# Two tables of slots instead of one: five expert blocks filled from the first twelve token tiles and run in pieces inside the last tiles' stages

## The chip, the cores and the metric

The kernel runs on one NeuronCore of a Trainium2 chip. The metric is the device time of one execution in microseconds. The engines are named as in the profile: PE is TensorE (PEld its weight loads), DVE is VectorE, ACT is ScalarE, POOL is GpSimd, SP is the sync engine, which here only issues DMAs. All data are float32.

## The reference, cut to what matters

The input is x (2, 1024, 256), so 2048 tokens of width 256, and a context ctx (2, 77, 256). Four residual sublayers follow each other, each behind a layer norm (`a` to `d` are the names that the kernel gives them).

```python
x = x + cross_attention(layernorm(x), ctx, ctx, mask)      # a: 16 heads of 16
x = x + routed_attention(layernorm(x))                     # b: 4 of 16 heads of 64, chosen per batch, 1024 keys
x = x + gelu(layernorm(x) @ ctx.T) @ ctx                   # c: feed-forward on the context
x = x + moe(layernorm(x))                                  # d

def moe(x):                                # E = 8 experts, H = 256, F = 1024
    logits = x @ w_router
    probs = softmax(logits); sel = argmax(probs); wgt = probs[sel]
    for e in range(8):
        h = relu(x @ w1[e] + b1[e])
        y = h @ w2[e] + b2[e]
        out += (sel == e) * wgt * y
```

Each token goes to one expert only. How many tokens an expert has is known only when all logits are there.

## The kernel before, in words

**Tiles.** A token tile is 128 tokens; there are T = 16, handled in groups of two (c and d stages) or in 32 steps of stage b (`b_step`, one step for a pair of heads and a stretch of queries). `xs[:, t, :]` holds the residual stream of tile t in SBUF.

**Order.** On PE, DVE, ACT and POOL the instructions run in the order in which the Python code issues them (`tc.manual_schedule`). A small plan places side work inside the steps of stages a and b: `at(stage, step, pos, f, args)` registers a call, and `take` runs it at that position. Only SP, the DMA queue of weights and of the rows written to DRAM, is ordered by the tile framework's scheduler. Waits between engines are inserted by the framework from the tiles that instructions read and write.

**Stages c and d inside b.** When the queries of a group of two tiles are through stage b, its group runs c and d some steps later: `do_rows("c")` (layer norm: statistics on DVE, the power −1/2 on POOL, the rows y on POOL or DVE), `do_turn` (transposes on PE), `c_hidden`, `c_gelu`, `c_out`, then the same for d, where the rows y and xs also go to a DRAM table `ztok` of 2 × 256 numbers a token, then `d_logits` (PE) and `d_expert` (DVE: argmax as a one-hot `oh`, running counts `seen`). The last group, tiles 14 and 15, ends after the last b step.

**Table of slots.** With all 16 tiles through d, two matmuls (`rank_ps`, L1051 and L1055) give every token's rank within its expert and the counts. DVE turns them into the number of 128-token blocks of each expert, the block's expert (`eidi`), and each token's slot (L1061 to L1145). 16 one-hot matmuls (`tok_ps`, L1124; each shows as two records in the profile) invert this into lists: for each block slot its token (`tok`) and weight (`swgt`). Experts' last blocks may be partly empty; at most NB = 23 blocks arise, 20 always run, and the rest stand in an If.

**Expert blocks.** `pipeline(range(used), block_loads, block_hidden, block_out)` runs the blocks as a three-stage pipeline: in one step the weights of block n + 2 are asked for, block n + 1 does its hidden part, and block n its output part.

- `block_loads` (L1151): w1s and w2s (1 MB each) and b2s (128 KB, the bias spread over partitions) on SP, and zb, an indirect gather of 128 rows of `ztok`, on POOL. Three buffers for weights, four for zb.
- `block_hidden` (L1172): the block's bias b1s, two transposes of zb (`ybps`), a copy (`ybT`), then 8 × 2 matmuls into one PSUM tile `ph` of 128 × 1024 (f counts the 8 slices of 128 hidden units), then eight relus from `ph` into `ehT`:

```python
        for f in range(FC):
            for c in range(C):
                nc.tensor.matmul(
                    ph[:, f, :], lhsT=ws[n][0][:, c, f * P : (f + 1) * P], rhs=ybT[:, c, :],
                    start=(c == 0), stop=(c == C - 1),
                )
        for f in range(FC):
            if f < FC // 2:
                nc.scalar.activation(hT[:, f, :], ph[:, f, :], AF.Relu, bias=b1s[:, f : f + 1])
            else:
                nc.vector.tensor_scalar(hT[:, f, :], ph[:, f, :], b1s[:, f : f + 1], 0.0, ALU.add, ALU.max)
```

- `block_out` (L1202): 8 matmuls of `ehT` by w2s into `epo` (128 × 256), two DVE operations into `ob` (bias, then weight and residual), and an indirect scatter of `ob` to the output on POOL.

A matmul of the program shows as two records on PE in the profile. PSUM has three pools of two buffers: `big` (ph), `trp` (transposes), `accp` (epo and most others).

Of the kernel before, what the change touches and what calls it, by code (L numbers as in the profile page):

```python
# [39 lines left out]
def kernel(  # L40
# [55 lines left out]

    const = ctx.enter_context(tc.tile_pool(name="const", bufs=1))
# [7 lines left out]
    work = ExitStack()  # L105
    ytp = work.enter_context(tc.tile_pool(name="ytp", bufs=2))
    ynp = work.enter_context(tc.tile_pool(name="ynp", bufs=6))
    ap_ = work.enter_context(tc.tile_pool(name="ap_", bufs=2))
    wsp = work.enter_context(tc.tile_pool(name="wsp", bufs=1))
    qkp = work.enter_context(tc.tile_pool(name="qkp", bufs=2))  # L110
    stage_a = ExitStack()
    rawp = stage_a.enter_context(tc.tile_pool(name="rawp", bufs=1))
# [7 lines left out]
        nm: rawp.tile([P, C, D], F32, name=f"raw_{nm}") for nm in "qkvo"  # L120
# [11 lines left out]
    def bcast_load(name, ap, n):  # L132
        t = const.tile([P, n], F32, name=name)
        nc.sync.dma_start(t, bcast_rows(ap, n))
        return t

    def col_load(name, ap):
        t = const.tile([P, C], F32, name=name)
        with nc.allow_non_contiguous_dma(reason="bias columns"):
            nc.sync.dma_start(t, ap.rearrange("(c p) -> p c", p=P))  # L140
        return t
# [7 lines left out]
    mask_i = const.tile([P, B, KC], I32, name="mask_i")  # L149
# [6 lines left out]
    bv_b = bcast_load("bv_b", a_bv, D)  # L156
# [3 lines left out]
    bo_b = bcast_load("bo_b", a_bo, D)  # L160
# [28 lines left out]
    hmask = const.tile([P, HG], F32, name="hmask")  # L189
# [12 lines left out]
    hsel = const.tile([P, NCH, H], F32, name="hsel")  # L202
# [15 lines left out]
    hwin = const.tile([P, NCH, HW], F32, name="hwin")  # L218
# [3 lines left out]
    neg3 = const.tile([P, 1], F32, name="neg3")  # L222
# [10 lines left out]
    ones16 = const.tile([P, P], BF16, name="ones16")  # L233
# [45 lines left out]
    def ln_rows(tag, t0, bias=None, y_out=None, last=False):  # L279
# [4 lines left out]
        nc.gpsimd.tensor_tensor(rs, rs, minus_half, ALU.pow)  # L284
        ys = []
        for i in range(2):
            y = ynp.tile([P, D], F32, name=f"y_{tag}_{t0 + i}", tag="y")
            (nc.vector if last else nc.gpsimd).tensor_scalar(  # L288
                y, xs[:, t0 + i, :], mv[:, i, 0:1], rs[:, i : i + 1], ALU.subtract, ALU.mult
            )  # L290
            ys.append(y)
            if y_out is not None:
                r0 = (t0 + i) * P
                nc.sync.dma_start(y_out[r0 : r0 + P, :D], y)
                nc.sync.dma_start(y_out[r0 : r0 + P, D:], xs[:, t0 + i, :])
        if bias is not None:
            add_bias(t0, 2, bias)
# [35 lines left out]
    def turn_weight(nm):  # L333

        t = wT[nm] = const.tile([P, C, D], F32, name=f"w{nm}T")
# [9 lines left out]
    keep01 = const.tile([P, B, KC], F32, name="keep01")  # L345

    mneg = const.tile([P, B, HG, KC], BF16, name="mneg")

    kblk = const.tile([P, B, C, HG, KC], F32, name="kblk")

    def context_k(m):
# [9 lines left out]
        kT = small.tile([P, B, KC], F32, name=f"kT_{m}", tag="kT")  # L361
# [6 lines left out]
    vc = const.tile([KC, B, D], F32, name="vc")  # L368
    pick = const.tile([KC, 3, KC], F32, name="pick")
    nc.gpsimd.tensor_copy(pick, ident[:KC, :KC].unsqueeze(1).to_broadcast([KC, 3, KC]))  # L370
    vblk = const.tile([P, B, NCH, HW, HD + 1], F32, name="vblk")
# [168 lines left out]
    def route_mean(b):  # L540
        ys = small.tile([P, C], F32, name=f"yt_{b}", tag="yt")
        nc.vector.tensor_reduce(ys, sel[b], AX.X, ALU.add)
        ym = sel[b] = small.tile([P, C, P], F32, name=f"ym_{b}", tag="ym", bufs=1)
# [17 lines left out]
    def route_heads(b):  # L561
# [54 lines left out]
        hot = small.tile([P, NA, NH], F32, name=f"hot_{b}", tag="hot", bufs=1)  # L616
# [4 lines left out]
        hb = small.tile([P, 2, NA, NH], F32, name=f"hb_{b}", tag="hb", bufs=1)  # L621
# [4 lines left out]
        hs_ = small.tile([P, 2, NP, 2], F32, name=f"hs_{b}", tag="hs", bufs=1)  # L626
# [10 lines left out]
    def b_qk(b, k, m, n):  # L637

        w, bc, _ = sel[b]
        if (b, k, m) not in qks:  # L640
            qks[b, k, m] = qkp.tile([P, S], F32, name=f"{k}T_{b}_{m}", tag=f"{k}T{m}")
        ps = accp.tile([P, 512], F32, name=f"bps_{b}_{m}_{k}_{n}", tag="acc")
# [8 lines left out]
        return lambda: nc.scalar.activation(  # L651
# [4 lines left out]
    def b_v(b, t):  # L656
        w, _, bv = sel[b]
        if b not in vs:
            vs[b] = qkp.tile([P, NT, NA, FD], F32, name=f"v_{b}", tag="v")
        ps = trp.tile([P, NA, FD], F32, name=f"vbps_{b}_{t}", tag="tr")  # L660
# [151 lines left out]
    def c_gelu(t0):  # L812
# [3 lines left out]
        nc.scalar.activation(g, ps, AF.Square)  # L816
        nc.vector.scalar_tensor_tensor(g, g, 1 / GELU_C, ps, ALU.add, ALU.mult)
        nc.scalar.activation(g, g, AF.Tanh, scale=math.sqrt(2 / math.pi) * GELU_C)
        nc.vector.scalar_tensor_tensor(g, g, 1.0, ps, ALU.add, ALU.mult)
# [25 lines left out]
    emx = keep.tile([P, T], F32, name="emx")  # L845
    TE2 = [P, 2, E]
    lps = {}

    def d_logits(t0):
        yT = yTs.pop(("d", t0))  # L850
        ps = lps[t0] = accp.tile([P, 2, E], F32, name=f"elps_{t0}", tag="acc")
        for i in range(2):
            for c in range(C):
                nc.tensor.matmul(
                    ps[:, i, :], lhsT=yT[:, c, i * P : (i + 1) * P], rhs=wrt_s[:, c, :],
                    start=(c == 0), stop=(c == C - 1),
                )

    def d_expert(t0):

        ts_ = slice(t0, t0 + 2)
        nc.vector.tensor_copy(logits[:, ts_, :], lps.pop(t0))
# [25 lines left out]

    rows = {}
# [9 lines left out]
    def do_rows(tag, t0, *args):  # L899
        rows[tag, t0] = ln_rows(tag, t0, *args)  # L900

    def do_turn(tag, t0, pool=trp, ptag="tr"):

        b, n = t0 // NT, t0 % NT * P
        if tag in "ab":
            if (tag, b) not in yTs:
                yTs[tag, b] = ytp.tile([P, C, S], F32, name=f"yT_{tag}{b}", tag="yT")
# [6 lines left out]
    def do_qk(*args):  # L914
        b_qk(*args)()
# [43 lines left out]
    for s, args in (  # L959
# [3 lines left out]
        at("a", s, 3, do_qk, *args)  # L963
    at("b", 3, 3, do_qk, 0, "q", 0, 512)
    at("b", 5, 3, do_qk, 0, "q", 1, 512)
    for t in range(NT):
        at(*(("a", 18, 3), ("a", 18, 3), ("b", 0, 3), ("b", 0, 3),
             ("b", 1, 0), ("b", 1, 3), ("b", 2, 0), ("b", 2, 3))[t], b_v, 0, t)
    for s, pos, args in (
        (6, 3, ("k", 0, 0)), (7, 2, ("k", 0, 512)), (8, 2, ("q", 0, 0)), (9, 2, ("k", 1, 0)),  # L970
        (9, 3, ("k", 1, 512)), (10, 3, ("q", 1, 0)), (17, 2, ("q", 0, 512)), (21, 2, ("q", 1, 512)),
    ):
        at("b", s, pos, do_qk, 1, *args)
    for t in range(NT):
        at("b", 8 + t, 0, b_v, 1, t)

    for g in range(T // TG):
        s, t0, last = 4 * g, TG * g, g == T // TG - 1
        at("b", s + 8, 3, do_rows, "c", t0, None, None, last)
        at("b", s + 10, 0, do_turn, "c", t0)  # L980
        at("b", s + 10, 2, c_hidden, t0)
        at("b", s + 10, 3, c_gelu, t0)
        at("b", s + 11, 2, c_out, t0)
        at("b", s + 11, 3, do_rows, "d", t0, None, ztok, last)
        at("b", s + 12, 2, do_turn, "d", t0, accp, "acc")
        at("b", s + 13, 2, d_logits, t0)
        at("b", s + 13, 3, d_expert, t0)
    at("b", 30, 3, d_probability, 0, NT)

    with tc.manual_schedule(  # L990
# [43 lines left out]
        ebp = work.enter_context(tc.tile_pool(name="ebp", bufs=2))  # L1034
# [5 lines left out]
        for s in range(NI + PR, NI + PR + 16):  # L1040
            for pos in (0, 2, 3):
                take("b", s, pos)
        assert not plan, plan
        d_probability(NT, NT)
    work.close()


    rp = ctx.enter_context(tc.tile_pool(name="rp", bufs=1))

    ps = accp.tile([P, T + 1, E], F32, name="rank_ps", tag="acc")  # L1050
    nc.tensor.matmul(  # L1051
        ps.rearrange("p t e -> p (t e)"), lhsT=ones, rhs=seen.rearrange("p t e -> p (t e)"),
        start=True, stop=False, skip_group_check=True,
    )
    nc.tensor.matmul(  # L1055
        ps[:, :T, :].rearrange("p t e -> p (t e)"), lhsT=upper,
        rhs=oh.rearrange("p t e -> p (t e)"),
        start=False, stop=True, skip_group_check=True,
    )

    gt = rp.tile([P, E, T], F32, name="egt")  # L1061
    nc.vector.tensor_tensor(
        gt, ps[:, T, :].unsqueeze(2).to_broadcast([P, E, T]),
        iota128[:, :T].unsqueeze(1).to_broadcast([P, E, T]), ALU.is_gt,
    )
    nblk = rp.tile([P, E], F32, name="enblk")
    nc.vector.tensor_reduce(nblk, gt, AX.X, ALU.add)
    earlier = rp.tile([P, E, E], F32, name="eearlier")
    nc.vector.tensor_tensor(
        earlier, tri, nblk.unsqueeze(1).to_broadcast([P, E, E]), ALU.mult  # L1070
    )
    start = rp.tile([P, E], F32, name="estart")
    nc.vector.tensor_reduce(start, earlier, AX.X, ALU.add)
    end = rp.tile([P, E], F32, name="eend")
    nc.vector.scalar_tensor_tensor(end, nblk, float(P), start, ALU.mult, ALU.add)

    le = rp.tile([P, NB, E], F32, name="ele")
    nc.vector.tensor_tensor(
        le, end.unsqueeze(1).to_broadcast([P, NB, E]),
        iota128.unsqueeze(2).to_broadcast([P, NB, E]), ALU.is_le,  # L1080
    )
    eid = rp.tile([P, NB], F32, name="eid")
    nc.vector.tensor_reduce(eid, le, AX.X, ALU.add)
    nc.vector.tensor_scalar(eid, eid, float(E - 1), None, ALU.min)
    eidi = rp.tile([P, NB + 1], I32, name="eidi")
    nc.vector.tensor_copy(eidi[:, :NB], eid)
# [183 lines left out]
```

## Time and profile before

| what | us |
|---|---|
| median of three runs | 659.47 (658.7 to 661.55) |
| the profiled execution's own time | 659.47 |
| its span | 657.7 |
| PE busy | 585.8 (89%) |
| DVE busy | 342.9 (52%) |
| ACT busy | 234.5 (36%) |
| POOL busy | 168.8 (26%) |
| DMA moved | 62.72 MB, of which the 20 blocks' weights are 43.8 MB |
| last b step's projection ends | 457.2 |
| table of slots on DVE | 478 to 484.4 |
| first expert transpose | 501.2 |
| last epo matmul ends | 650.0 |

The span runs from the first to the last instruction of the profiled execution; 1.8 us of its time lie around it. Busy time of an engine counts its instructions, not their waits. The idle figure of a group is the idle time of its engine just before its instructions, with what ended it. The chain is the work that ended last, followed back from the end. PEclk is the clock that TensorE was granted, as a share of full speed.

### The profile page before, as it was taken

How to read it: one execution, taken by the hardware profiler on the slowest of the kernel's cores; microseconds unless marked ns; L12 is line 12 of the kernel's file. 1: busy time of each engine (PE TensorE's matmuls, PEld its weight loads, DVE VectorE, ACT ScalarE, POOL GpSimd, SP SyncE). 2: the span in 40 equal slices, each digit the busy share in tenths (PEclk: the TensorE clock that was granted, in tenths of full speed). 3: DMA queues.
4: the chain of work that ended last, by engine and by line, in shares of the span. 5: the costliest groups of instructions: out<-in, count | busy, mean ns of one | idle time of the engine just before them, and what ended most of it. 6: DMA issues, size and time to landing. Idle time of an engine off the chain costs nothing.

```text
span 657.7 us, 9891 instructions
## 1 busy us (share of the span) xinstructions
PE 585.8 (89%) x3662; PEld 425.2 (65%) x3662; DVE 342.9 (52%) x842; ACT 234.5 (36%) x475; POOL 168.8 (26%) x210
## 2 busy tenths in 40 slices
PE   5999999898899999999989999875455999999995
PEld 4678778775555555655555555543345999999894
DVE  6767668925574536665746666623351333323331
ACT  3555456433465344453535454510100121112110
POOL 6655222243000201222120403132022323223221
PEclk9999999999899999999989999985556999999999
DMA  8000000110002000000000000000158799999980
GB/s 246 6 1 1 1 1 1 29 28 1 1 5 53 1 0 33 1 21 13 17 17 16 17 17 17 17 16 32 33 201 296 248 330 350 362 361 348 351 308 13
DMA packets 49671, 62.72 MB, mean 95 GB/s; under 512 B 11512, under 2 KB 42707, under 8 KB 49621
## 3 DMA queue, kind: packets, MB, share of 16 engines
q1 hardware_dynamic: 46352, 54.04, 24.7%
q0 software_dynamic: 2560, 7.34, 3.2%
q10 hardware_dynamic: 709, 0.68, 0.3%
q8 instruction: 30, 0.49, 0.3%
q14 instruction: 20, 0.16, 0.1%
HBM read 55.76 MB, written 6.82 MB: 95 GB/s over the span
## 4 chain that ended last, share of the span: by engine, by line
PE 75%; DVE 7%; POOL 6%; issue 4%; ACT 2%; DMA 2%; POOLq 0%; ACTq 0%; DVEq 0%
PE ph L1190 11%; PE epo L1207 10%; PE bov L729 9%; PE bpt L719 8%; PE bsc L693 8%; PE av L468 4%; PE sc L421 3%; POOL y_d L288 3%; PE vbps L662 2%; PE po_b L761 2%; PE pt L459 2%; DMA zb<-ztok,etok 2%; PE qps L323 2%; PE po_a L492 1%; PE gpo L825 1%
## 5 line engine op out<-in xcount | busy, mean ns | idle before, releaser
L707 DVE TENSOR_REDUCE bnm<-bsc 128x1 f32<-128x1024 f32 x64 | 75.2, 1217 | 13.4 <-PE bsc L693 13.3
L719 PE MATMUL bpt<-ident,be 128*128 128x128 f32 x512 | 72.8, 281 | 6.6 <-DVE beT L720 3.2
L719 PEld LDWEIGHTS bpt<-ident,be 128*128 128x128 f32 x512 | 55.6, 141 | 33.6 <-issue 10.2
L720 DVE COPY beT<-bpt 128x512 f32<-128x512 f32 x64 | 43.8, 686 | 63.0 <-PE bpt L719 63.0
L1190 PE MATMUL ph<-ybT,w1s 128*128 128x128 f32 x640 | 76.5, 279 | 0.0
L1190 PEld LDWEIGHTS ph<-ybT,w1s 128*128 128x128 f32 x640 | 74.5, 195 | 2.8 <-DVE ybT L1185 2.2
L1207 PE MATMUL epo<-w2s,ehT 128*128 128x256 f32 x320 | 75.2, 379 | 0.0
L1196 ACT ACTIVATE ehT<-ph,b1s 128x128 f32<-128x128 f32 x80 | 22.8, 368 | 145.1 <-issue 105.9
L709 ACT ACTIVATE be<-bsc,bnm 128x1024 f32<-128x1024 f32 x64 | 70.8, 1111 | 10.4 <-DVE bnm L707 9.8
L1198 DVE TENSOR_SCALAR ehT<-ph,b1s 128x128 f32<-128x128 f32 x80 | 22.5, 345 | 93.7 <-ACT ehT L1196 93.7
L720 ACT COPY beT<-bpt 128x512 f32<-128x512 f32 x64 | 37.5, 585 | 90.1 <-PE bpt L719 89.5
L729 PE MATMUL bov<-beT,v 128*64 128x256 f32 x512 | 65.6, 401 | 1.5 <-ACT qT L651 1.5
L693 PE MATMUL bsc<-kT,qT 64*128 64x512 f32 x256 | 64.9, 618 | 0.0
L1207 PEld LDWEIGHTS epo<-w2s,ehT 128*128 128x128 f32 x320 | 57.9, 190 | 6.4
L729 PEld LDWEIGHTS bov<-beT,v 128*64 128x64 f32 x512 | 35.2, 141 | 25.4 <-issue 9.9
L741 POOL COPY brb<-brc 128x256 f32<-128x256 f32 x16 | 6.3, 397 | 158.2 <-DVE brc L739 158.2
L1216 POOL DMA_INDIRECT out_dram<-ob,etok x20 | 20.3, 1013 | 81.9 <-DMA out_dram<-ob,etok 68.3
L693 PEld LDWEIGHTS bsc<-kT,qT 64*128 64x128 f32 x256 | 22.5, 188 | 27.1 <-issue 24.5
L468 PE MATMUL av<-vblk,eT 128*128 128x51 f32 x320 | 37.4, 272 | 0.9 <-DVE hn L476 0.9
L468 PEld LDWEIGHTS av<-vblk,eT 128*128 128x128 f32 x320 | 37.1, 192 | 1.6 <-DVE hn L476 1.1
L444 DVE TENSOR_REDUCE mx<-sc 128x8 f32<-128x616 f32 x32 | 25.4, 793 | 16.4 <-PE sc L430 16.4
L460 ACT COPY eT<-pt 128x512 f32<-128x512 f32 (+1 forms) x48 | 23.0, 515 | 25.9 <-PE pt L459 25.1
(233 smaller groups left out, 840.5 us busy)
## 6 DMA issues: line engine op xcount, KB each, us to landing
w1s<-in_L_ffn_w_dram SPq DMA_DIRECT2D x20, 1024.0 KB
w2s<-in_L_ffn_w_dram SPq DMA_DIRECT2D x20, 1024.0 KB
b2s<-in_L_ffn_b_dram SPq DMA_DIRECT2D x20, 128.0 KB
xs<-in_x_dram SPq DMA_DIRECT2D x4, 512.0 KB
ztok<-xs SPq DMA_DIRECT2D x16, 128.0 KB
ztok<-y_d SPq DMA_DIRECT2D x16, 128.0 KB
ws_k<-in_L_ffn_Wk_dram SPq DMA_DIRECT2D x8, 64.0 KB
ws_q<-in_L_ffn_Wq_dram SPq DMA_DIRECT2D x8, 64.0 KB
```

The lines of the kernel that those rows point to most:

```text
L444: nc.vector.tensor_reduce(mx, scv, AX.X, ALU.max)
L460: copy(eTs[t][:, c0 : c0 + n, :], pt[:, :n, :])
L468: nc.tensor.matmul(av[:, h0 : h0 + HW, :].rearrange("p h d -> p (h d)"), lhsT=eT[:, c, :], rhs=vblk[:, t // NT, c].rearrange("p h d -> p ( ...
L693: nc.tensor.matmul(sc[h][:, n : n + 512], lhsT=qks[b, "q", m][r, q0 : q0 + P], rhs=qks[b, "k", m][r, n : n + 512], start=True, stop=True,)
L707: nc.vector.tensor_reduce(nm, sc[h], AX.X, ALU.max, negate=True)
L709: nc.scalar.activation(bes[i][:, h], sc[h], AF.Exp, bias=nm, accum_out=sms[g][:, q, s : s + 1])
L719: nc.tensor.transpose(pt[:, k - k0, :], bes[i][:, h, k * P : (k + 1) * P], ident)
L720: copy(beTs[gm][:, h, k0 : k0 + 4, q * P : (q + 1) * P], pt)
L729: nc.tensor.matmul(ovs[gm][h * FD : (h + 1) * FD, :], lhsT=vs[g * TG // NT][:, k, 2 * m + h, :], rhs=beTs[gm][:, h, k, :], start=(k == 0), ...
L1190: nc.tensor.matmul(ph[:, f, :], lhsT=ws[n][0][:, c, f * P : (f + 1) * P], rhs=ybT[:, c, :], start=(c == 0), stop=(c == C - 1),)
L1196: nc.scalar.activation(hT[:, f, :], ph[:, f, :], AF.Relu, bias=b1s[:, f : f + 1])
L1207: nc.tensor.matmul(po, lhsT=hT[:, f, :], rhs=w2s[:, f, :], start=(f == 0), stop=(f == FC - 1))
```

## The change

The one table of slots becomes two.

- **First table, from tiles 0 to 11** (T1 = 12). Whatever the routing, 12 tiles fill at least K1 = 5 whole blocks of one expert each. After the logits of tiles 10 and 11 (now at b step 32) `first_blocks` (step 33, position 2) and `first_tokens` (step 35, position 0) build a table of exactly five whole blocks and gather their rows. Tokens that are left over wait for the second table.
- **Second table, from all 16 tiles**, with NB − K1 = 18 slots, for the tokens that the first didn't take.
- **Ranks group by group.** `d_rank` adds to the logits' PSUM tile the ranks of the group before (two matmuls); `d_split` splits a rank into its block and its row in it; `d_row` builds the one-hot rows of the list matmuls early, some inside stage b.
- **Blocks as a generator.** `blocks()` yields after every pair of ph matmuls with its relu, and after every epo matmul: 16 pieces a block. `tail()` yields how many pieces to run between two of its own steps, which are the c and d stages of tiles 12 to 15, their logits, and the second table. The pipeline of before is gone: hidden of block n, then transposes of block n + 1 (`block_turn`), then out of block n.
- **Order inside a block.** `block_hidden` issues the relu of f directly behind the two matmuls of f, in turn on DVE (even f) and ACT (odd f). This holds for all 20 blocks.
- **Loads.** Blocks 0 to 4 take weights from a pool `w1p` of two buffers, the others from `w2p` of four, which takes the place of stage b's buffers when the last group is through. The weights of block n + 2 (first table) or n + 4 (second) are asked for at the beginning of block n. `block_rows` gathers zb, five buffers; hp has two buffers for the rest.
- SBUF is split into pools by lifetime (`early`, `late`, `acon` for constants of stage a) with some on the right side; `ln_rows` is split into `ln_power` and `ln_rows`; the rows y of the last groups' layer norms go to DVE; a few other calls of the plan move by a step.

The core of the diff:

```diff
+    T1 = 12
+    K1 = -(-(T1 * P - E * (P - 1)) // P)
...
+        if t0:
+            d_rank(t0 - 2, ps[:, 1])
...
+    def d_rank(t0, ps):
+        nc.tensor.matmul(ps.rearrange("p t e -> p (t e)"), lhsT=ones,
+            rhs=seen[:, t0 : t0 + 2, :].rearrange("p t e -> p (t e)"), start=True, stop=False)
+        nc.tensor.matmul(ps.rearrange("p t e -> p (t e)"), lhsT=upper,
+            rhs=oh[:, t0 : t0 + 2, :].rearrange("p t e -> p (t e)"), start=False, stop=True)
...
+    def block_hidden(n):
+        ph = big.tile([P, FC, P], F32, name=f"ph_{n}", tag="big")
+        hT = hTs[n] = pools["h"].tile([P, FC, P], F32, name=f"ehT_{n}", tag="ehT")
+        ybT, b1s = ybTs.pop(n), b1ss.pop(n)
+        for f in range(FC):
+            for c in range(C):
+                nc.tensor.matmul(
+                    ph[:, f, :], lhsT=ws[n][0][:, c, f * P : (f + 1) * P], rhs=ybT[:, c, :],
+                    start=(c == 0), stop=(c == C - 1),
+                )
+            if f % 2:
+                nc.scalar.activation(hT[:, f, :], ph[:, f, :], AF.Relu, bias=b1s[:, f : f + 1])
+            else:
+                nc.vector.tensor_scalar(
+                    hT[:, f, :], ph[:, f, :], b1s[:, f : f + 1], 0.0, ALU.add, ALU.max
+                )
+            yield
...
+    def blocks():
+        block_turn(0)
+        for n in range(used):
+            if 2 <= n + 2 < K1:
+                block_loads(n + 2)
+            if n >= K1 and n + 4 < used:
+                block_loads(n + 4)
+            yield from block_hidden(n)
+            if n + 1 < used:
+                block_turn(n + 1)
+            yield from block_out(n)
+            next_rows.append(n + ZB)
+            rows_due()
...
+    def first_blocks():
+        d_counts(T1)
+        ps = cps[T1]
+        d_split(T1 - 2, ps[:, :2])
+        every(d_blocks(T1, K1))
+        block_loads(0)
+        block_loads(1)
+        d_row(T1 - 2, 2, nc.vector)
+        d_probability(NT, T1 - NT)
+        every(d_slots(T1, K1))
+
+    def first_tokens():
+        d_tokens(T1, K1)
+        d_lists(T1, K1)
+        for n in range(K1):
+            block_rows(n)
+
+    at("b", 33, 2, first_blocks)
+    at("b", 35, 0, first_tokens)
...
+    def tail():
+        t1 = T - 2
+        do_power("c", t1)
+        d_logits(T1)
+        yield 1
+        do_y("c", t1)
+        d_expert(T1)
+        yield 2
...
+        late_stages_done()
+        for n in range(K1, K1 + 4):
+            block_loads(n)
...
+        d_lists(T, NB - K1)
+        rows_due()
...
+        pieces = blocks()
+        for n in tail():
+            for _ in range(n):
+                next(pieces)
+        every(pieces)
...
-    used = (B * S) // P + E // 2
-    slots = nc.values_load(eidi[0:1, NB : NB + 1], min_val=P, max_val=NB * P)
-    pipeline(range(used), block_loads, block_hidden, block_out)
```

## Prediction

> **What bounds the kernel now.** I read the page's slices first, then the stretches around the table of slots, then the chain of waits, then the groups of the expert blocks. In the slices (40 of 16.4 us), two places show TensorE below full use: slices 28 to 31, where its clock is also halved, and the last.
>
> ```profile
> PE   5999999898899999999989999875455999999995
> DVE  6767668925574536665746666623351333323331
> PEclk9999999999899999999989999985556999999999
> ```
>
> The stretches put times on that hole (columns: window, length, busy time and instructions of PE, PEld, DVE, ACT, POOL, granted clock, DMA share, GB/s).
>
> ```profile
> 450.00:460.00 10.00, 4.59 (x16) 3.74 (x16) 3.15 (x13) 0.58 (x1) 3.85 (x4) 0.50 0.12 41
> 460.00:470.00 10.00, 5.15 (x12) 2.70 (x12) 4.46 (x18) 1.38 (x3) 0.00 (x0) 0.50 0.05 14
> 470.00:480.00 10.00, 4.21 (x16) 3.41 (x16) 4.32 (x23) 0.84 (x2) 0.69 (x1) 0.50 0.12 41
> 480.00:490.00 10.00, 5.58 (x27) 5.61 (x27) 6.38 (x22) 0.00 (x0) 2.98 (x6) 0.50 0.67 220
> 490.00:500.00 10.00, 1.46 (x7) 1.29 (x7) 0.68 (x5) 0.00 (x0) 4.07 (x4) 0.50 1.03 371
> 510.00:520.00 10.00, 10.00 (x66) 9.16 (x66) 2.62 (x9) 2.28 (x8) 2.39 (x4) 1.00 0.52 166
> ```
>
> From the last attention work (457.3, the residual add of the last b step) to the first expert transpose (501.2) nothing but small dependent steps runs: the last group's c and d stages, the table on VectorE, its lists, a gather. Into those 44 us the change puts work. Behind them the chain of waits (start, length, what) shows the blocks:
>
> ```profile
> 484.43 7.04 PE tok_ps L1124 x32
> ...
> 492.51 1.23 POOL zb L1165
> ...
> 494.04 7.13 DMA zb<-ztok,etok
> ...
> 514.20 0.87 PE epo L1207 x4
> 515.07 3.60 PE ph L1190 x32
> 518.67 2.59 PE epo L1207 x12
> 521.26 0.22 PE ybps L1183 x2
> ```
>
> Only PE is on the chain there: a block is .87 + 3.60 + 2.59 + .22 = 7.28 us with no gap, at full clock. Why relu never shows is in the groups (busy and mean ns, then idle before and its releaser):
>
> ```profile
> L1190 PE MATMUL ph<-ybT,w1s 128*128 128x128 f32 x640 | 76.5, 279 | 0.0
> L1207 PE MATMUL epo<-w2s,ehT 128*128 128x256 f32 x320 | 75.2, 379 | 0.0
> L1196 ACT ACTIVATE ehT<-ph,b1s 128x128 f32<-128x128 f32 x80 | 22.8, 368 | 145.1 <-issue 105.9
> L1198 DVE TENSOR_SCALAR ehT<-ph,b1s 128x128 f32<-128x128 f32 x80 | 22.5, 345 | 93.7 <-ACT ehT L1196 93.7
> ```
>
> PE waited 0.0 us ahead of ph and epo. ScalarE's relu starts only when all 32 ph records of its block are over (one block: ph ends 525.95, relu starts 526.04), though the first of its eight slices was ready 3 us earlier, and VectorE's four start when ScalarE's four are done (93.7 us of idle, all by that releaser). So waits on ph and ehT go by the whole tile, not by the slice. It costs nothing here: epo of the block before lies on PE meanwhile.
>
> [...] the changes at 429.72, 433.12, 446.77 and 504.8 lie on one 3.413 us grid. [...] here windows with PE busy 22, 44, 51 and 62% were each followed by half clock, others of 58 to 64% were not, and full clock came back only after windows with 100%.
>
> **The change part by part.** (1) *First table.* Five blocks are filled from tiles 0 to 11, and run between the last group's c and d stages, the logits and the second table. Taken alone it moves 5 × 7.28 = 36.4 us of PE work into the 44 us hole. The table work moves to steps 33 to 35 of stage b: ranks are taken two tiles at a time in d_logits (4 records, N = 16), d_split adds 1.3 to 1.5 us of VectorE a group (six small ops; such ops take .06 to .26 in the chain), d_blocks about 3, d_slots about 2.8. They stand on VectorE among the last steps' copies, which are on the path there (PE 4.59 us in ten at 450), and five gathers of zb on POOL (1.0 us each plus .3 issue = 6.3) stand ahead of the last layer norms' powers, for which y, its ztok stores on SP, and the c and d turns wait. The first expert matmul cannot come before the last b projection (457.2) and the gather after the first lists; I take 463 ± 8 (low end: the added work hides and tiles 0 to 11 are early; high end: VectorE's and POOL's additions all lie on the path).
>
> (2) *Order inside block_hidden, in all 20 blocks.* Before: 16 matmuls, then four relus on ScalarE, four on VectorE. After: two matmuls into ph[:, f, :], at once their relu, then the next two. Since waits go by the tile, the pair of f + 1 must wait for the relu of f, which reads the same tile. The instruction order of the changed kernel says so: in one block the pairs f = 1 to 7 wait in turn for VectorE, ScalarE, VectorE and so on, each time one relu further, where before no ph matmul after the first waited. Seven round trips a block. The price of one, from single records: four records of N = 128 from start to end .61 to .66 us at full clock (1.11 to 1.16 at half); PE end to start on ScalarE or VectorE .03 to .09; relu .368 or .345; relu end to next matmul .13 (ybT ends 514.77, matmul 514.90). Together 1.17 us at full clock and 1.72 at half, against .45 for four records that stream (3.60 / 8). ACT and DVE relus don't overlap, nor does epo fill the gaps: the order in PE is hidden(n), turn(n + 1), out(n), and epo's last waits for the last relu.
>
> Hidden: 7 × 1.17 + .45 = 8.64. On VectorE the two ob operations (.42 and .48) of block n − 1 stand ahead of the first relu: + .35. Block at full clock: 8.64 + .35 + 3.46 + .22 = **12.7 us**. At half throughout: 7 × 1.72 + .9 + 2 × 3.68 = **20.3**.
>
> (3) *Clock.* In hidden PE is then busy .61 of 1.17 us, 52%: beside the windows above, more likely dropped than not. Out at half clock is 16 records × .43 = 6.9 us without a gap, two windows, so it holds a whole busy one and wins the clock back. A block then starts fast, turns slow after the first whole window inside hidden (on average 5.1 us in), and turns fast again 5.1 us into out. Hidden: 5.1 + (8.99 − 5.1) × 1.72 / 1.17 = 10.8; out: 5.1 + (7.4 − 5.1) / 2 = 6.2; sum 17. The grid can fall better; I take **16.3**, within 15.5 to 17.5.
>
> (4) *Tail.* Two c/d groups and the second table put about 22 us of VectorE work (two d_expert of 3.1, splits, d_blocks, d_slots, eblk, lists, y, powers) between relus of the first blocks. Where relus are on the path, it is on the path: + 22. If they weren't, about + 10 for its PE work and turns.
>
> (5) *Loads.* On SP, w1s of block 4 comes behind all weights of blocks 5 to 8, since only two w1p buffers serve the first table. [...] 5 blocks × 2.23 MB at some 355 GB/s (slices 34 to 38 of the page moved 348 to 362) are 31 us after block 1 ends; blocks 2 and 3 must last that long. At 12.7 they cover all but 5, at 16.3 all, at 7.28 all but 16. Bufs, pools on the right side, b1s and ybT made earlier: nothing, hidden under 3.5 us of epo.
>
> **Sum.** 463 + 20 × 16.3 + 22 + 8 (last epo to the span's end, 650.0 to 657.7 before) = 819 us of span; + 1.8 outside it (before: 659.47 − 657.7, a run that is also the median of the three shown) = 821. As the start may be earlier than 463 and a few tail ops fit into PE's waits, I say **817**.
>
> **Rivals.** *Full clock kept* (.25): 52% suffices. 463 + 254 + 22 + 8 + 1.8 + 5 = 754. For: windows of 58% kept it. Against: 51% lost it. *Never won back* (.10): relu waits break the windows so that none is full: 463 + 406 + 22 + 9.8 = 901. Against: 6.9 us of unbroken out. *The wait is cheap or absent, and the hole is filled* (.05, the one that ends on the other side): pairs overlap relus in place of waiting. Then 463 + 20 × 7.28 + 10 + 9.8 + 16 = 645. It decides at B ≈ 7.8 us a block (463 + 20B + 15 + 9.8 + 31 − 2B = 659.5), thus at (7.8 − 3.68 − .45) / 7 = .52 us a pair; the records of a pair alone take .61, and a relu must follow. That the change doesn't do what it says: the five blocks could start only at the second table's time, which adds to a slow kernel and changes no sign.
>
> **How the numbers follow.** Mixed clock .60: its own range 775 to 860 (B 15.5 to 17.5 is ± 20, the start ± 8, the tail 10 to 22; lower if the clock is kept in some blocks). For 8 in 10 the range reaches down into the full-clock case and leaves out most of the always-half and the cheap one: 735 to 865. Faster by over .5% (3.3 us, about what a measurement of this kernel can tell from no change): .04; within it .01; slower .95.
>
> **What would show it.** Right: after ph, relu and PE in turn on the chain in every block; PE idle before ph of 5 us or more a block with the relus as releasers; ph's sum of idle 100 us or more; PEclk of .5 to .8 in the last third; first ph near 463; DMA share falling below .5 in the steady blocks. Wrong: ph with 0.0 idle; a block below 8 us; a clock of 1.0 in the blocks (then the full-clock case); or a stretch of over 10 us in which PE waits for w1s of block 4.

## The result, and the profile after

The changed kernel takes 805.5 us (median of 4 runs, 798.1 to 811.7) against 660.4 us (median of 4 runs of the kernel before): a ratio of 1.216, interval 1.205 to 1.228. By the medians it is slower by some 145 us; the ratio leaves out the slowest of the four runs (811.7), which counts as a slow one. The profiled execution took 801.9 us, its span is 800.2. The forecast was 817, within 735 to 865.

The page of the changed kernel, its slices (40 of 20 us):

```profile
PE   6999999999999999999986777876778767777874
PEclk9999999999999999999997675676897797779778
DMA  7000002002000000000002623692355454454000
```

The hole of the kernel before no longer stands out, but from slice 22 on PE is busy only 6 to 8 tenths and its clock swings to the very end. DMA, which had been full under the expert blocks (9 tenths in slices 33 to 38 of the page before), is at about half (4 to 5 tenths in slices 30 to 37): the weights are no longer what is close behind.

The groups of the expert blocks (busy and mean ns, then the engine's idle time before them and what ended most of it):

```profile
L1131 PE MATMUL ph<-ybT,w1s 128*128 128x128 f32 x640 | 139.5, 352 | 79.9 <-DVE ehT L1138 47.6
L1136 ACT ACTIVATE ehT<-ph,b1s 128x128 f32<-128x128 f32 x80 | 29.4, 367 | 289.2 <-PE ph L1131 286.0
L1149 PE MATMUL epo<-w2s,ehT 128*128 128x256 f32 x320 | 103.8, 494 | 0.0
L1138 DVE TENSOR_SCALAR ehT<-ph,b1s 128x128 f32<-128x128 f32 x80 | 27.9, 349 | 141.6 <-PE ph L1131 141.6
```

Three things changed. PE waited 0.0 us ahead of ph before; now it waits 79.9, of which 75.0 end with a relu (47.6 on DVE, 27.4 on ACT). DVE's relus waited for ACT's before; now both wait for PE. And epo, which nobody touched and which waits for nothing, went from 379 to 494 ns a record: that is clock (e4 below, with the clock back, has 386). A relu itself costs what it did, 367 and 349 ns.

The chain of waits in one block shows the turn-taking (start, length, what; a block at full clock):

```profile
652.56 0.44 DVE ob L1154
...
653.02 0.48 DVE ob L1156
653.50 0.28 DVE ehT L1138
653.78 0.04 issue
653.82 0.73 PE ph L1131 x4
...
654.58 0.04 issue
654.62 0.38 ACT ehT L1136
655.00 0.04 issue
655.04 0.73 PE ph L1131 x4
...
657.02 0.38 ACT ehT L1136
657.39 0.04 issue
657.44 0.73 PE ph L1131 x4
...
661.77 0.22 PE ybps L1121 x2
661.99 3.47 PE epo L1149 x16
...
665.49 0.44 DVE ob L1154
```

PE, ACT, PE, DVE: each four records, a pair of matmuls, wait for the relu of the four before. From one pair to the next it is 1.17 to 1.23 us (653.82 to 655.04, for one). The pair at 657.44 is the fifth, the first in the other half of ph, and it too waits for the relu of the fourth: the wait goes by the whole tile. The first relu of the block stands behind the two ob operations of the block before. From ob to ob this block takes 12.93 us.

Most blocks take more. The stretches below are cut every 3.413 us: the clock's changes in this trace lie whole multiples of that apart (it fell at 670.75, rose at 680.99, fell at 687.82: 3 and 2 of them). The cuts lie .15 us ahead of the changes, hence the .52 and .98 (columns: length; busy time and instructions of PE, PEld, DVE, ACT, POOL; granted clock; DMA share; GB/s):

```profile
667.19:670.60 3.41, 1.93 (x13) 1.36 (x12) 0.35 (x1) 0.73 (x2) 1.87 (x3) 1.00 0.99 329
670.60:674.01 3.41, 2.44 (x10) 1.85 (x10) 0.35 (x1) 0.37 (x1) 0.00 (x0) 0.52 0.26 103
674.01:677.43 3.42, 2.90 (x12) 2.50 (x11) 0.90 (x3) 0.37 (x1) 0.00 (x0) 0.50 0.00 0
677.43:680.84 3.41, 3.41 (x9) 2.70 (x8) 0.00 (x0) 0.00 (x0) 0.00 (x0) 0.50 0.95 305
680.84:684.25 3.41, 2.55 (x15) 2.12 (x13) 1.17 (x3) 0.00 (x0) 0.57 (x1) 0.98 0.18 45
684.25:687.67 3.42, 1.94 (x13) 1.38 (x12) 0.35 (x1) 0.73 (x2) 1.76 (x3) 1.00 0.98 331
```

A window inside hidden at full clock has PE busy 1.93 of 3.41 us, 57%. After it the clock is half. The next two windows, 71 and 85% busy, don't win it back; the one that lies wholly in epo, 3.41 of 3.41, does. Then it starts again, after five windows: 17.07 us, close to the length of these blocks (16.96 from ob to ob).

### The profile page after: what moved, and what is told of

Same layout as the page of the kernel before. It is cut to its first block, busy times and chain, and to the rows that moved or that the text cites. A ratio compares the mean times of both kernels' runs of the same rounds, so it can differ in the third digit from the quotient of the medians.

```text
span 800.2 us, 10199 instructions
## 1 busy us (share of the span) xinstructions
PE 680.0 (85%) x3722; PEld 487.2 (61%) x3722; DVE 363.9 (45%) x939; ACT 240.7 (30%) x476; POOL 161.7 (20%) x204
## 4 chain that ended last, share of the span: by engine, by line
PE 70%; DVE 10%; issue 8%; ACT 4%; SPq 3%; POOL 2%; DMA 1%; DVEq 0%; ACTq 0%; POOLq 0%
PE ph L1131 13%; PE epo L1149 10%; PE bpt L728 7%; PE bsc L702 7%; PE bov L738 7%; PE av L477 3%; DVE ehT L1138 3%; SPq L1096 2%; ACT ehT L1136 2%; PE sc L430 2%; PE pt L468 2%; PE bps_q L653 2%; PE qps L332 2%; PE po_b L770 2%; PE vbps L671 2%
## 5 line engine op out<-in xcount | busy, mean ns | idle before, releaser
L1131 PE MATMUL ph<-ybT,w1s 128*128 128x128 f32 x640 | 139.5, 352 | 79.9 <-DVE ehT L1138 47.6
L1131 PEld LDWEIGHTS ph<-ybT,w1s 128*128 128x128 f32 x640 | 106.7, 234 | 112.5 <-DVE ehT L1138 64.8
L1136 ACT ACTIVATE ehT<-ph,b1s 128x128 f32<-128x128 f32 x80 | 29.4, 367 | 289.2 <-PE ph L1131 286.0
L1149 PE MATMUL epo<-w2s,ehT 128*128 128x256 f32 x320 | 103.8, 494 | 0.0
L1138 DVE TENSOR_SCALAR ehT<-ph,b1s 128x128 f32<-128x128 f32 x80 | 27.9, 349 | 141.6 <-PE ph L1131 141.6
L1149 PEld LDWEIGHTS epo<-w2s,ehT 128*128 128x128 f32 x320 | 81.9, 264 | 15.8
L728 PEld LDWEIGHTS bpt<-ident,be 128*128 128x128 f32 x512 | 55.6, 140 | 28.3 <-issue 10.1
L738 PEld LDWEIGHTS bov<-beT,v 128*64 128x64 f32 x512 | 35.1, 142 | 25.3 <-issue 10.5
L1154 DVE TENSOR_TENSOR ob<-epo,b2s 128x256 f32<-128x256 f32 x20 | 8.5, 424 | 84.8 <-PE epo L1149 84.8
```

Of the source, the lines that this page charges most:

```text
L728: nc.tensor.transpose(pt[:, k - k0, :], bes[i][:, h, k * P : (k + 1) * P], ident)
L738: nc.tensor.matmul(ovs[gm][h * FD : (h + 1) * FD, :], lhsT=vs[g * TG // NT][:, k, 2 * m + h, :], rhs=beTs[gm][:, h, k, :], start=(k == 0), ...
L1131: nc.tensor.matmul(ph[:, f, :], lhsT=ws[n][0][:, c, f * P : (f + 1) * P], rhs=ybT[:, c, :], start=(c == 0), stop=(c == C - 1),)
L1149: nc.tensor.matmul(po, lhsT=hT[:, f, :], rhs=w2s[:, f, :], start=(f == 0), stop=(f == FC - 1))
```

## The experiments

The theory: waits on the PSUM tile ph go by the whole tile, so the new order makes seven round trips PE, relu, PE in each block, and the gaps also lose the clock. Rivals: the two tables and what they move (VectorE work, loads) are the cost; or the relus are slow in themselves; or the clock has nothing to do with the gaps. Block lengths below are from one ob to the next in the profiled execution, in the steady part.

### e1 and e5: the relu order in the kernel with one table

In the kernel before, the two edits of e1 were the relu directly behind its pair, and the block pipeline inside a hand-ordered part. The second edit is needed because, unlike the stages ahead of them, the expert blocks of before stand outside `tc.manual_schedule`: there the framework's scheduler places instructions of neighbouring blocks between each other (hence epo x4, ph x32, epo x12 on the chain of before). It could have filled the waits.

```diff
         for f in range(FC):
             for c in range(C):
                 nc.tensor.matmul(ph[:, f, :], ...)
-        for f in range(FC):
-            if f < FC // 2:
+            if f % 2:
                 nc.scalar.activation(hT[:, f, :], ph[:, f, :], AF.Relu, ...)
...
-    pipeline(range(used), block_loads, block_hidden, block_out)
+    with tc.manual_schedule(engines={PE, DVE, Activation, Pool}):
+        pipeline(range(used), block_loads, block_hidden, block_out)
```

> The kernel before (one table, all blocks after all tiles), with two edits: the relu of f directly behind its two ph matmuls, in turn on DVE and ACT, and the block pipeline in the order of the code (hidden n+1, then out n) on PE, DVE, ACT and POOL. Theory (seven round trips through ph a block, and the clock that they lose): about 16 us a block as in the changed kernel, so 501 + 20 x 16.4 + 10 = 839 us (full clock kept: 785). Rival (the two tables, their VectorE work and loads cost the time, the order of the relus nothing): within 10 us of 660, or about 680 if the fixed order alone costs 1 us a block.

Measured: 956.6 us (ratio 1.455, 1.448 to 1.461), a block 22 to 23 us. The rival of this run, that the order costs nothing, is out; but 956 is far over the theory's 839. The waits of PE in e1 say why (waited for: us in total, times, longest):

```profile
PE ph L1190 <- DVE ybT L1185: 78.1, 20, 4.4
PE ph L1190 <- DVE ehT L1197: 40.6, 80, 0.9
PE ph L1190 <- ACT ehT L1195: 28.3, 60, 0.5
```

The fixed order made a chain of its own: on POOL the scatter of ob stands ahead of the gather and of b1p for the next block, DVE's ybT stands behind b1s, and PE waits for it some 4 us a block (78.1 / 20; 4.4 at most). So a control was needed: e5, which is e1 without the relu edit.

> The control for e1: the kernel before with only the fixed order of the block pipeline on PE, DVE, ACT and POOL; all 16 ph matmuls of a block, then its eight relus, as before. In e1 a chain ob, scatter, gather, b1p, b1s, ybT held PE 4.4 us a block apart from the relus; it should stand here too. Theory: 7.28 + 4.4 = 11.7 us a block, 501 + 20 x 11.7 + 10 = 745 us, up to 790 if the gaps cost clock; e1 less this run, over 20 blocks, is the price of the relu order: 8 to 10 us a block. Rival (fixed order is what made e1 slow): above 900.

Measured: 772.9 us (1.168, 1.157 to 1.178), a block 13.49 us. The same wait is there, and no wait for a relu:

```profile
L1190 PE MATMUL ph<-ybT,w1s 128*128 128x128 f32 x640 | 108.2, 348 | 80.2 <-DVE ybT L1185 80.2
```

What follows: with one table, no tail and the same loads, the relu order alone costs (956.6 − 772.9) / 20 = 9.2 us a block, of which the waits for relus are (40.6 + 28.3) / 20 = 3.4. The slower records of epo (501 ns in e1, 379 in e5) show that lost clock is in the rest; how much of it was not measured.

### e8: the old relu order in the changed kernel

The smallest undoing: everything of the change stays but the place of the relus.

```diff
-            if f % 2:
-                nc.scalar.activation(hT[:, f, :], ph[:, f, :], AF.Relu, ...)
-            else:
-                nc.vector.tensor_scalar(hT[:, f, :], ph[:, f, :], ...)
-            yield
+            if f < FC - 1:
+                yield
+        for f in range(FC):
+            if f < FC // 2:
+                nc.scalar.activation(hT[:, f, :], ph[:, f, :], AF.Relu, ...)
+            else:
+                nc.vector.tensor_scalar(hT[:, f, :], ph[:, f, :], ...)
+        yield
```

> The changed kernel with the old order inside block_hidden alone: 16 ph matmuls of one tile, then four relus on ACT, four on DVE; hidden, transposes and out of a block still follow each other. Theory: one round trip a block in place of eight; PE waits once for the relus, 8 relus one after the other are 2.9 us less .2 of transposes (epo's first needs only the first relu, its last all eight, so part is hidden), a block is 7.8 to 10 us: 503 + 18 x 9 + 10 + 18 (weights of block 4) = 690, range 670 to 712. Rival (the lost overlap of hidden and out of neighbouring blocks is the main cost): above 750.

Measured: 675.4 us (ratio to before 1.021, 1.011 to 1.030). 130 of the 145 us are back. A block takes 7.80 us. In the groups:

```profile
L1131 PE MATMUL ph<-ybT,w1s 128*128 128x128 f32 x640 | 78.4, 282 | 22.4 <-DMA w1s<-in_L_ffn_w_dram 21.9
L1152 PE MATMUL epo<-w2s,ehT 128*128 128x256 f32 x320 | 77.9, 396 | 5.9 <-ACT ehT L1139 5.9
```

PE waits .3 us a block for the first relu, and no more. In one block the first relu ends at 597.08, epo starts at 597.13, and the other seven relus run beside it until 599.01: the waits of epo on ehT go by the slice, not by the tile. I had reckoned with 7.8 to 10 and taken 9. The lost overlap of hidden and out between neighbouring blocks costs at most half a microsecond a block (7.80 for 7.28), so the rival of this run is out too. The 21.9 us is one wait, for the weights of block 4.

### e2 and e3: the same blocks without the shared tile

e2 keeps the order of every instruction and changes only which tile it writes: even f in one PSUM tile and one SBUF tile (DVE's), odd f in another (ACT's).

```diff
-        ph = big.tile([P, FC, P], F32, name=f"ph_{n}", tag="big")
+        phs = [big.tile([P, FC // 2, P], F32, name=f"ph{i}_{n}", tag="big") for i in range(2)]
...
-                    ph[:, f, :], lhsT=...
+                    phs[f % 2][:, f // 2, :], lhsT=...
```

> The changed kernel, order of all instructions kept, but ph and ehT are each two tiles, one for even f (DVE's relus), one for odd f (ACT's): the pair f+1 no longer shares a tile with the relu of f, only pair f+2 does. Theory: a round trip of 1.17 us then carries two pairs, hidden falls from 8.6 to about 4.9 us, PE is busy enough for full clock, a block is about 9 us, and the run 490 + 18 x 9 + 10 + 13 (weights of block 4) = 675 us. Rival (relus or their engines are slow in themselves, or the tables are the cost): 790 to 810.

Measured: 682.5 us (1.038, 1.034 to 1.042), a block 8.47 us, at full clock once the tail and one wait for weights are over (the clock in its slices, then the group of ph):

```profile
PEclk9999999999999999999999999768696699999999
```

```profile
L1133 PE MATMUL ph<-ybT,w1s 128*128 128x128 f32 x640 | 98.1, 302 | 31.4 <-DMA w1s<-in_L_ffn_w_dram 21.7
```

This is the cleanest test of the wait: relus in the same places, on the same engines, as many. Only the shared tile is gone, and with it 123 us. (ehT is split along with ph; but the matmuls that waited write only ph.)

e3 puts four slices into each of two tiles; the four relus of a half follow its eight matmuls.

```diff
+            if f % H2 == H2 - 1:
+                for g in range(f - H2 + 1, f + 1):
+                    o, i = hT[g // H2][:, g % H2, :], phs[g // H2][:, g % H2, :]
+                    if g % H2 < H2 // 2:
+                        nc.scalar.activation(o, i, AF.Relu, ...)
+                    else:
+                        nc.vector.tensor_scalar(o, i, ...)
```

> The changed kernel with ph and ehT in two tiles of four slices each; the four relus of a half (two on ACT, two on DVE) stand behind its eight matmuls, so PE streams the second half while the first is read. Theory: no round trip is left on PE, a block is 7.3 us as before the change. The last groups' chain of c, d and second table (30 to 35 us) then covers blocks 0 and 1, and block 4 waits some 16 us for weights that come behind those of blocks 5 to 8: 490 + 18 x 7.3 + 16 + 10 = 647 us, a little below 660. Rival (the first table and the tail cost more than the hole gives): above 665.

Measured: 669.0 us (1.015, 1.012 to 1.019), a block 7.25 us, with PE never waiting for a relu. The block is as theory has it; the run is 22 us over the theory's 647, on the rival's side of 665. Two terms were too small. The weights of block 4 are waited for 22.4 us instead of 16 (PE's waits):

```profile
PE ph L1134 <- DMA w1s<-in_L_ffn_w_dram: 22.4, 1, 22.4
PE lps_d L320 <- DVE y_d L299: 6.6, 2, 4.4
PE tok L1046 <- DVE eblk L1036: 5.5, 1, 5.5
```

And the tail with blocks 0 and 1 ends at 502.9, not 490: its own chain of small steps leaves PE idle for 10.5 of the 43 us from 460 to 503 (5.5 for eblk, 2.3 of the 6.6 for y_d) at a mean clock of .78. So with a sound block only two of the first table's five blocks lie in the old hole, and the table gives more than that back in one wait for loads.

### e4: useless work in the waits

The changed kernel, with two more matmuls of the same operands behind each pair but the last, into a PSUM tile that nobody reads.

```diff
+            if f < FC - 1:
+                for c in range(C):
+                    nc.tensor.matmul(fill[:, c, :], lhsT=ws[n][0][:, c, f * P : (f + 1) * P],
+                                     rhs=ybT[:, c, :], start=True, stop=True)
             if f % 2:
```

> The changed kernel with useless PE work in the waits: behind the two ph matmuls of each f (but the last) two more of the same operands go to a spare PSUM tile that nobody reads (7 x 4 records a block). They need .45 us at full clock and lie inside the .56 us in which PE waits for the relu. Theory (the waits cost twice, once as idle time, once as lost clock): the granted clock stays near 1.0, a block takes 12.9 us in place of 15.5, and the run is faster by 16 x 2.6 and some 8 in the tail: about 755 us, although PE does 25% more work. Rival (the clock does not follow PE's busy share): not faster than 800; more work only adds.

Measured: 759.2 us (1.154, 1.149 to 1.159), 46 us faster than the changed kernel, and every steady block 12.92 or 12.93 us. The clock in its slices, then the groups of PE:

```profile
PEclk9999999999999999999999867989699999999999
```

```profile
L1131 PE MATMUL ph<-ybT,w1s 128*128 128x128 f32 x640 | 115.2, 304 | 27.7 <-DMA w1s<-in_L_ffn_w_dram 12.1
L1139 PE MATMUL fill<-ybT,w1s 128*128 128x128 f32 x560 | 88.9, 283 | 0.0
L1157 PE MATMUL epo<-w2s,ehT 128*128 128x256 f32 x320 | 75.0, 386 | 0.0
```

88.9 us of added matmuls make the kernel faster. The round trips are all still there; epo is back at 386 ns. This separates the two halves of the cost: against e3 the round trips take 12.92 − 7.25 = 5.7 us a block at full clock, and lost clock takes another (792.2 − 506.5 − 3.4) / 18 − 12.9 = 2.8 on the mean of blocks 2 to 19. Over 18 blocks that is 50 us, of which a longer wait for block 4's weights (12.1 us for 3.4) takes back 9.

### e6 and e7: the order of the loads, and fuller waits

e6 is e3 with the requests of the second table spread, so that block 4's weights come ahead of those of 6, 7 and 8:

```diff
-            if n >= K1 and n + 4 < used:
+            if n >= 2 and n + 4 < used:
                 block_loads(n + 4)
...
-        for n in range(K1, K1 + 4):
-            block_loads(n)
+        block_loads(K1)
```

> e3 (ph and ehT in halves) with one more edit: at the second table only block 5's weights are asked for, block 4's next, and those of 6, 7, 8 at the beginning of blocks 2, 3, 4. In e3 PE waited 22.4 us once for w1s of block 4. Theory: that wait goes, 669 - 22 = 647 us. Rival (the bytes are what is late, in any order): the wait moves to a later block, 660 to 669.

Measured: 648.6 us (ratio to before .977, .968 to .986). PE's wait for w1s fell from 22.4 to 3.1 us, and no other took its place: the bytes are the same, the order was at fault.

e7 is e6 with `yield 6` for `yield 1` ahead of the turn of the last d rows, and `yield 13` for `yield 1` ahead of the second table's list matmuls.

> e6 with 17 more pieces of blocks put where PE waited in the tail of e3: 5 before the turn of the last d rows (2.3 us of wait), 12 before the list matmuls of the second table (5.5 us). Theory: 17 x .45 us of block work move into waits, about 640 us. Rival (VectorE and the other dependent steps set the tail's length, and the added relus lengthen it): as e6, within 3 us.

Measured: 631.5 us (.952, .943 to .960), better than the 640 expected. Its slices:

```profile
PE   5999999999999999999999999977788999999994
PEclk9999999989999999999999999996689799999998
```

And PE's longest waits:

```profile
PE lps_d L320 <- DVE y_d L299: 3.7, 1, 3.7
PE epo L1153 <- DVE ehT L1144: 2.6, 1, 2.6
```

The waits for eblk (5.5 us) and for w1s (3.1) are gone. The gain on e6 is 17.1 us. From 460 to 503 PE is idle 5.7 us less (4.8 for 10.5), and 3.1 are the wait for w1s; beside them the first ph starts 2.8 us earlier (457.9 for 460.7), and the mean clock from 460 to 500 is .89 for .80. How the rest splits was not tested. This version beats both kernels, the one before by some 30 us (662.1 beside it).

## Why the prediction was right

**The bound and the wait.** The reading that carried it was that ACT's relu of before began only at the end of the last ph record. It said that ph is waited for as a whole, and the changed order turned that into seven waits a block. e2 and e8 show it from two sides. One part of the reading was wrong: I wrote that waits on ehT go by the tile as well. On ehT epo's waits go by the slice (e8). That leaves ph, which both engines read, as the reason why DVE's relus of before waited for ACT's; no run splits ph without ehT, so this is inferred. Nothing in the sum hung on it, but it made my expectation for e8 too long.

**The price of a round trip.** 1.17 us at full clock and 1.72 at half were forecast; 1.21 and 1.71 measured, as means over blocks 5 to 19 (1.68 and 1.74 in turn at half clock). The block at full clock was to be 12.7 and is 12.93.

**The clock.** Forecast: dropped by a window inside hidden at 52% busy, won back in epo. Measured: dropped at 54 to 59%, won back in epo. That 52% would lose the clock was a bet on the windows of before, where 51 and 62% had lost it and 58% kept it, and it came out. But the busy share alone does not decide: in e5 windows of 44 to 50% kept full clock, so the reason was weaker than the result. The block of 17 us on average alignment was right for half of the last fourteen blocks; I had leant to 16.3, and the mean over blocks 2 to 19 without the wait for loads is 15.7. In the other seven the grid falls better: three pass at full clock throughout (12.93), four at 14.4 to 14.6.

**The sum, term by term** (profiled execution): first ph 457.4, forecast 463; blocks 0 and 1 with the tail's work 49.1 (to 506.5), forecast 54.6; the other eighteen blocks 282.3 (506.5 to 792.2 less 3.4), forecast 293.4; wait for block 4's weights 3.4, forecast none at this block length; rest 8.0, forecast 8. Together 800.2 against 819. The larger terms were all a little high, so their misses add up in place of cancelling.

**The start.** That 457.4 lies near the low end of 463 ± 8 is in part luck. I took the last b projection to end at 457.2, as before; in the changed kernel it ends at 448.5, and the first ph comes 8.9 us behind it. Why stage b ends earlier was not tested. The chain shows the gap: the d stage of tiles 12 and 13 and their logits stand on PE ahead of the first block.

```profile
445.06 1.72 PE po_b L770 x4
...
448.37 3.10 issue
451.47 0.43 DVE y_d L299
...
451.94 1.02 PE lps_d L320 x4
...
457.40 1.24 PE ph L1131 x4
```

In the 3.10 us that the chain calls issue, POOL runs the last two of the five gathers, until 450.68; only then comes the power that y_d needs, whose input was ready at 448.51. So the gathers did hold the start back, by some 2 us, as the high end of the forecast allowed; the earlier end of stage b made up for it.

**Loads.** That block 4's weights come behind those of blocks 5 to 8 was read off the order on SP, and e6 bears it out (with the order changed, the wait for them fell from 22.4 us to 3.1); how long that takes was not read rightly: from the end of block 1 to block 4's weights it took 36.6 us in the changed kernel and 38 in e3, where I reckoned 31 from bytes and rate. (The bytes were right: 2.23 MB a block make 44.6 MB for twenty, where the table of the profile before has 43.8.) Slow blocks hid it; every version with sound blocks brought it out (21.7 to 22.4 us in e2, e3 and e8).

**What I had said would show it.** Turn-taking on the chain: there. PEclk between .5 and .8 in the last third: slices of mostly 7 tenths, some of 9. DMA below .5 in the steady blocks: 4 to 5 tenths. Two signs were set too high: PE's idle ahead of ph was to be 5 us a block or more and 100 us in all, and is 79.9 / 20 = 4.0. My own round trip gave no more: 7 × (1.17 − .61) = 3.9.

**The other side.** The rival that ended faster asked for pieces that cost no more than they stream. e3, e6 and e7 are that case made: 669 with the wait for loads, where it said 645, and 649 and 631 without. Its block was right, its tail (+ 10) and its wait (16) were too short.

## What to carry to other kernels

Before interleaving a producer and a consumer more finely, find out by what unit the wait between them goes: if by the tile, cut the tile along with the work, or every piece becomes a round trip (seven of 1.21 us a block here). Price a gap on PE twice, once as time and once as clock (5.7 and 2.8 us a block here), and look for a stretch of unbroken matmuls that would win the clock back (here the windows of epo with PE busy 3.41 of 3.41 us). When work is moved ahead of other work, read the load queue in its new order, since a slow stage can hide a late load that the repaired one will wait for (3.4 us of wait in the changed kernel, 22.4 in e3).

## What the runs showed of the hardware that I had not expected

In the changed kernel gaps of half a microsecond cost the clock. Cut on the clock's own changes (670.75 is one), the windows of 3.413 us between 507 and 790 fall into clear groups. At full clock, fourteen windows with PE busy 54 to 59%, none with a gap over .56 us, were followed by half clock, and so was the one that holds the wait for weights; 31 windows of 59% or more kept it. At half clock, 22 windows of 70 to 85% did not win it back, and fifteen of 100% did.

This edge is one of this kernel's blocks and not a rule. In e5 windows of 44 to 50% kept full clock (569.4 to 572.8 and 596.7 to 600.1), with one gap of 1.7 to 1.9 us each, and in e1 a window of 85% at half clock (617.9 to 621.3) was followed by full clock. In the kernel before, four windows of 100% at half clock were followed by full clock, but the one from 487.75 to 491.16 was not. What counts beside the busy share stays open.

A block's length can come close to a multiple of these windows: 16.96 us against five of them, 17.07. The two slip against each other by .1 us a block: two or three such blocks follow each other, then a block of 14.6 and mostly one of 12.93 come between.

And useless matmuls paid: 88.9 us of them on PE took 46 us off the kernel.
